# Four-layer graph network, layer 3: a tile's attention logits in one run of four chunks, and another place for ScalarE's second measuring pass

## The chip, the cores and the metric

The kernel runs on one core of a Trainium2 chip, in one launch. The metric is the device time of one execution in microseconds (us), and the profile is that of one execution. The engines are called as in the profile: PE (TensorE's matmuls), PEld (its weight loads), DVE (VectorE), ACT (ScalarE), POOL (GpSimd) and SP (SyncE, which issues most DMAs).

## The reference

`x` is 3327 x 256, `adj` is 3327 x 3327, both float32. Four layers each add `f(relu(layernorm(x)), adj)` to x. Layers 0 to 2 are a plain propagation, a filtered one (tanh, top-k) and a normalised one. The change is in layer 3 alone, which takes two steps of a propagation and of an attention that is cut to the heaviest entries of each row:

```python
def _top_p_attention(X, W1, W2, W3):
    q = X @ W1.T @ W2.T            # 64 wide
    k = X @ W3.T                   # 64 wide
    probs = softmax(q @ k.T)
    # keep, row by row, the largest entries until their sum reaches 0.9
    A = probs * mask
    return A / A.sum(-1)

R = S + I;  R = R / R.sum(-1);  Xf = Xa = X;  Z = 0
for n in range(2):
    A = _top_p_attention(Xa, W1, W2, W3)
    Xf = R @ Xf
    Xa = A @ Xa
    Z = Z + Xf @ U1[n].T + Xa @ U2[n].T
return layernorm(X + Z) * ln_g + ln_b
```

## The kernel before

**Tiles.** The 3327 rows are padded to 3328 = 26 tiles of 128. In each of the two steps a tile passes through four stages.

1. *Logits* (`logits_steps`, L955). The keys lie in two halves of 13 tiles on partitions 0 to 63 and 64 to 127, so a logits matmul has 64-row weights and the two halves are computed by two matmuls side by side. The 13 x 128 = 1664 columns of a half are cut into `CHUNKS` of 512, 512, 512 and 128 (L953). Each chunk has a two-bank buffer of `ps_row` (two such buffers, L80), one bank per half. ScalarE's exp moves it into `e` and gives its sum into a column of `parts` (L983). The steps yield after chunk 1 and after chunk 3, so a tile's logits are two runs on PE.
2. *Search* (`search_steps`, L987). ScalarE sums the parts and works out a first threshold (L1000 to L1005), then measures the row with two passes over 3328 elements: a Relu (L1016) and a Sign (L1021). DVE turns both into a better threshold (L1026 to L1029), measures once more (L1032), collects candidates (L1041 to L1058) and then masks `e` (L1061) and takes the reciprocal `den` (L1065).
3. *Rows times values* (`rows_times_steps`, L177). PE transposes the masked `e` in groups of four blocks (L186) into a buffer of `ps_tr` (two one-bank buffers, L77), ScalarE copies each group to `eT` (L189), and PE multiplies it with the values (L197). `rows.begin` does the first two groups, `rows.finish` the rest.
4. *After the rows.* In step 1 ScalarE scales the result to `xa` (L1223). `turn` transposes it (L146; ScalarE's copy is recorded in `last_copied`), `node` makes the next step's keys and queries from it (L250), and `values` multiplies with U2 (L1236) into a `ps_row` buffer that ScalarE and DVE empty (L1242, `z` L1243). In step 2 ScalarE scales it to `y` (L1308), which POOL adds into z.

**Propagation.** Beside this, PE works off the product of R with the nodes, in phases of 39 or 52 matmuls of 128x128 (L1182; adjacency "slabs" of 832 KB come by DMA, and POOL adds the identity to a diagonal block, L1151). A pair of tiles has two phases.

**What sets the order.** All of this is emitted under `tc.manual_schedule(engines=PE_ALONE)` (L1435): PE's instructions run in the order in which they are emitted, and the Tile scheduler orders the other engines. Emission is steered by plans. A plan is a table from a place to functions; `run(steps, plan)` calls them when the steps have reached that place, and a propagation phase maps the places 0 to 25 onto its 39 or 52 matmuls. The logits of the tile three ahead (`AHEAD`) are hung into such a plan by `spread(steps, first=0, second=10)`, L1492: one run at each of two places. In step 1 most tiles are *interleaved* (a row stage, then a propagation phase; runs at 0 and 12). The tiles in `APART` (3, 7, 11, 15, 19) have no phase of their own, and their plan is that of `rows.finish`, with runs at 4 and 6. The first `EARLY` = 4 phases, and the last ones of step 1 (T - 3, T - 2, T - 1), have places of their own. In step 2 the runs are at 0 and 10 of the phase.

**ScalarE's passes.** `passes_apart` (L1459) puts the first pass (L1016) into `rows.finish` and the second (L1021) into the propagation phase that follows. `tc.issue_after(x)` makes the scheduler put it behind instruction x. The second pass is emitted at place 4 in step 1, behind the last copy of an `xT`, and at place 1 in step 2, behind the last exp issued so far, that is the exp of chunk 1.

Of the kernel before, what the change touches and what calls it, by code (L numbers as in the profile page):

```python
# [11 lines left out]
F32 = mybir.dt.float32  # L12
# [4 lines left out]
AF = mybir.ActivationFunctionType  # L17
# [4 lines left out]
N = 3327  # L22
D = 256
DA = 64
P = 128
T = 26
# [20 lines left out]
def kernel(  # L47
# [22 lines left out]
    nc = tc.nc  # L70
# [6 lines left out]
    ps_tr = ctx.enter_context(tc.tile_pool(name="ps_tr", bufs=2, space=PSUM))  # L77
    ps_acc = ctx.enter_context(tc.tile_pool(name="ps_acc", bufs=2, space=PSUM))

    ps_row = ctx.enter_context(tc.tile_pool(name="ps_row", bufs=2, space=PSUM))  # L80
# [52 lines left out]
    def merged(*plans):  # L133
        out = {}
        for p in plans:
            for k, v in p.items():
                out.setdefault(k, []).extend(v)
        return out

    last_copied, last_turned, last_exp, last_found = [], [], [], []  # L140

    def transposed(src, pool, name):

# [742 lines left out]
    def layer_3_in(tag, big, ep, w3, sm3, h3, kT0, ksum0, left, at_end):  # L886
# [64 lines left out]
            return mean  # L951

        CHUNKS = [(c, min(c + 512, LOW * P)) for c in range(0, LOW * P, 512)]  # L953

        def logits_steps(kT, q, e, name, evict):  # L955


            halves_of_e = e.rearrange("p (h n) -> p h n", h=2)
            for c, (a, b) in enumerate(CHUNKS):
                pl = ps_row.tile([P, 2, 512], F32, tag="row", name=f"pl_{name}_{c}")  # L960
                for h in range(2):
                    nc.tensor.matmul(  # L962
                        pl[:, h, : b - a], q[h * DA : (h + 1) * DA, :], kT[h * DA : (h + 1) * DA, a:b],
                        start=True, stop=True,
                    )
                evict(c, halves_of_e[:, :, a:b], pl[:, :, : b - a])
                if c == len(CHUNKS) - 1:
                    nc.gpsimd.memset(e[:, N:], 0.0)
                if c % 2:
                    yield c  # L970

        def scores(step, m, kT):

            name = f"{tag}{step}_{m}"
            e = ep.tile([P, NP], F32, tag="e", name=f"e_{name}")

            parts = sm3.tile([P, len(CHUNKS) + 1], F32, tag="parts", name=f"parts_{name}")
            nc.gpsimd.memset(parts[:, len(CHUNKS) :], -1.0)
            return e, parts, exp_of_logits(step, m, kT, e, parts)

        def exp_of_logits(step, m, kT, e, parts, name=""):
# [323 lines left out]
        def attention_of_second_step(m, acc, den, name):  # L1305
            y = w3.tile([P, D], F32, tag="xa", name=f"y_{name}")
            with tc.high_priority():
                nc.scalar.activation(y, acc[:, :D], AF.Copy, scale=den)  # L1308
            return y


# [111 lines left out]
        kT1, ksum1 = new_keys(f"1{tag}", big)  # L1423
        AHEAD = 3
# [8 lines left out]
        ORDER = [p + i * H for p in range(H) for i in range(2)]  # L1433

        with tc.manual_schedule(engines=PE_ALONE):  # L1435
# [3 lines left out]
            def prepare(step, m, kT):  # L1439
                made[m] = scores(step, m, kT)  # L1440
                return made[m][2]
# [17 lines left out]
            def passes_apart(step, finder):  # L1459


                if finder is None:
                    return {}, {}

                first = passes(finder)[0]

                def second():
                    with tc.issue_after((last_copied if step == 0 else last_exp)[-1].ins):
                        next(finder, None)
                    next(finder, None)  # L1470

                return {0: first}, {4 if step == 0 else 1: [second]}

            pairs, fs = {}, []

            def propagate_first(n, at):

                p, phase = divmod(n, 2)
                pair = pairs.setdefault(p, PropagatedPair(0, p, h3, ts))
                units = H * len((PHASES if p else FIRST_PHASES)[phase])  # L1480
                run(pair.steps(phase), {k * units // T: v for k, v in at.items()})
                if phase == (p == 0):
                    pair.half()
                if phase and n != T - 3 and n != T - 1:
                    rows_of_first(p)
# [3 lines left out]
                for i in range(2):  # L1489
                    props.append(PropagationOfFirstStep(p + i * H, rows[:, i, :]))  # L1490

            def spread(steps, first=0, second=10):  # L1492

                return {k: [lambda: next(steps, None)] for k in (first, second)}

            class Rows:

# [25 lines left out]
            for i in range(EARLY):  # L1523
                plan = {}
                if props:
                    p = props.pop(0)
                    plan = {6: [lambda: p.scale(last_exp)], 13: [p.turn], 20: [p.sums]}
                if i == 0:
                    left.pool, left.bank = (w3, "eT", 3), one_bank
                    propagate_first(0, dict(zip((20, 25), ([what] for what in left.stages))))  # L1530
                    mean0 = key_sum(kT0, ksum0, "0")
                elif i == 1:
                    steps = prepare(0, 0, kT0)
                    centred = {3: [lambda: centre(kT0, mean0(), "0")]}
                    propagate_first(1, merged(centred, spread(steps, 9, 19), plan))
                    run(find(0, 0, st0))
                else:
                    propagate_first(i, merged(spread(prepare(0, i - 1, kT0)), plan))
                    finder = find(0, i - 1, st0)
                    if i + 1 < EARLY:  # L1540
                        run(finder)
# [3 lines left out]
            propagated = iter(range(EARLY, T - LATE))  # L1545
            for m in range(T):
                interleaved = m + AHEAD < T and m not in APART
                plan, later = passes_apart(0, finder) if interleaved else (passes(finder), {})
                plan = merged(plan, left_over)
                if props:  # L1550
                    p = props.pop(0)
                    plan = merged(plan, {2 if interleaved else 1: [p.scale], 3: [p.turn], 5: [p.sums]})
                steps = iter(())
                if m + AHEAD < T and not interleaved:
                    def begin_logits():
                        nonlocal steps
                        steps = prepare(0, m + AHEAD, kT0)
                        next(steps)

                    plan = merged(plan, {4: [begin_logits], 6: [lambda: next(steps)]})  # L1560
                a = AttentionOfFirstStep(m, rows.finish(m, plan), dens.pop(m), f"{m}")
                if interleaved:
                    left_over = {}
                    steps = prepare(0, m + AHEAD, kT0)
                    after = {3: [a.turn], 9: [a.node], 18: [a.values], 20: [lambda: rows.begin(m + 1)]}
                    propagate_first(next(propagated), merged(spread(steps, 0, 12), after, later))
                elif m == T - 3:
                    left_over = {}
                    after = {1: [a.turn], 4: [a.node], 8: [a.values], 22: [lambda: rows.begin(m + 1)]}
                    propagate_first(T - LATE, after)  # L1570
                elif m + 1 < T:
                    rows.begin(m + 1)
                    a.turn()
                    left_over = {0: [a.node], 2: [a.values]}
                finder = find(0, m + AHEAD, st0) if m + AHEAD < T else None
# [11 lines left out]
            def first_flags():  # L1587
# [4 lines left out]
            steps = prepare(1, 0, kT1)  # L1592
            propagate_first(T - 3, {
                1: [a.turn], 3: [first_flags], 4: [a.node], 8: [a.values, sum_second],
                11: [centre_second], 19: [lambda: next(steps)], 24: [lambda: next(steps)],
            })
            first_e, first_parts = made[0][:2]
            steps_of_second = prepare(1, ORDER[1], kT1)
# [23 lines left out]
        with tc.manual_schedule(engines=PE_ALONE):  # L1622
# [1 line left out]
            run(find(1, 0, st1))  # L1624
            rows_of_first(H - 2)
            p = props.pop(0)
            propagate_first(T - 2, merged(spread(steps_of_second, 0, 6), {3: [lambda: p.scale(last_exp)], 8: [p.turn], 12: [p.sums]}))
            p = props.pop(0)
            second = find(1, ORDER[1], st1)

# [2 lines left out]
                    next(second)  # L1633

            plan = {0: [lambda: p.scale(last_exp)], 3: [p.turn], 8: [p.sums], 15: [lambda: next(second), pass_of_second], 19: [pass_of_second]}
            propagate_first(T - 1, merged(spread(prepare(1, ORDER[2], kT1), 4, 10), plan))
            run(second)
            finder = find(1, ORDER[2], st1)
            fs.append(new_nodes(f"fs{tag}")[:, :, :D])
# [15 lines left out]
            for i, m in enumerate(ORDER):  # L1655
                ahead = ORDER[i + AHEAD] if i + AHEAD < T else None
                plan, later = passes_apart(1, finder) if ahead else (passes(finder), {})
                if i == 0:
                    p, q = props
# [3 lines left out]
                    nc.sync.dma_start(gs, ln_g.partition_broadcast(P))  # L1663
                    nc.sync.dma_start(bs, ln_b.partition_broadcast(P))
                ys[m] = attention_of_second_step(m, acc, dens.pop(m), f"{m}")
                plan = spread(prepare(1, ahead, kT1)) if ahead else {}
                if i + 1 < T:
                    plan = merged(plan, {20: [lambda: rows.begin(ORDER[i + 1])]}, later)
                else:
# [113 lines left out]
```

## Time and profile before

| | |
|---|---|
| median of 3 runs | 2582.86 us (2580.24 to 2583.54) |
| profiled execution | 2582.32 us, of which the span of its instructions is 2580.5 us |
| mean granted PE clock | 0.994 |
| PE, DVE, ACT, POOL busy | 97%, 81%, 42%, 11% of the span |
| logits matmuls in the trace (L962) | 832, from 975.2 to 2482.6 us |
| their two groups' busy time on PE | 88.9 and 87.9 us |
| exps (L983) | 208, 177.8 us on ACT |
| second passes (L1021) | 50, 153.5 us on ACT |

Layers 0 to 2 last until about 960 us of the span. Step 1 of layer 3 follows until about 1850 us, and step 2 to the end.

How to read it: times are counted from the first instruction. A group of instructions is named by line, engine, operation and its operands, "out<-in", with buffer numbers left out. A wait names the instruction that ended it. Successive matmuls overlap in the records, so what a matmul costs PE is read from its start to the next one's start. A float32 matmul appears as two entries of PE.

### The profile page before, as it was taken

The page shows a single profiled execution, that of the slowest core. Times are in us where ns is not written, and L with a number is a line of the kernel's source. Part 1 is how long each engine was busy: PE and PEld are TensorE (multiplying, and loading weights), DVE is VectorE, ACT ScalarE, POOL GpSimd, SP SyncE. Part 2 cuts the span into 40 slices and gives each one's busy share as a digit, 9 for nine tenths or more (in the row PEclk, how much of TensorE's full clock was granted, in tenths as well). Part 3 has the DMA queues.
Part 4 walks back from the last instruction along what each step waited for, and adds up shares of the span by engine and source line. Part 5 has one row for each costly group of instructions (what it writes and reads, how often), then busy time and mean ns, then how long its engine had stood idle before and what let it go on. Part 6 is the DMA issues. An engine that isn't in the chain of part 4 may idle for free. (4 is left out here: it accounts for less than half of the span.)

```text
span 2580.5 us, 47702 instructions
## 1 busy us (share of the span) xinstructions
PE 2514.0 (97%) x17929; PEld 2255.6 (87%) x17929; DVE 2082.3 (81%) x5538; ACT 1083.7 (42%) x2055; POOL 293.1 (11%) x485
## 2 busy tenths in 40 slices
PE   7999999999999999999999999998999999999997
PEld 7999999999999998878787878787888888888886
DVE  6667788888878778787778787784899899899994
ACT  3110123343111115555656566653555555555551
POOL 2000010000000001000000000000021122212132
PEclk9999999999999999999999999999999999999999
DMA  6677765555788865323232323232433343344342
GB/s 222 191 227 249 220 197 182 166 173 171 250 294 269 280 208 186 107 65 107 69 103 92 107 67 102 61 113 97 159 119 106 112 135 111 112 141 130 106 135 84
DMA packets 181794, 388.47 MB, mean 151 GB/s; under 512 B 19742, under 2 KB 78747, under 8 KB 181531
## 3 DMA queue, kind: packets, MB, share of 16 engines
q1 hardware_dynamic: 153210, 364.31, 43.7%
q10 hardware_dynamic: 28320, 20.80, 2.5%
q8 instruction: 147, 2.41, 0.4%
q14 instruction: 117, 0.95, 0.1%
HBM read 315.44 MB, written 67.89 MB: 149 GB/s over the span
## 5 line engine op out<-in xcount | busy, mean ns | idle before, releaser
L189 ACT COPY eT_a<-pt_a 128x512 f32<-128x512 f32 (+1 forms) x364 | 195.8, 554 | 361.2 <-PE pt_a L186 361.0
L197 PE MATMUL a<-h3a,eT_a 128*128 128x256 f32 x1352 | 325.7, 383 | 0.2 <-ACT eT_a L189 0.2
L197 PE MATMUL a<-vs,eT_a 128*128 128x256 f32 x1352 | 320.3, 381 | 0.2 <-ACT eT_a L189 0.2
L1045 DVE MAX8 cand_a<-w 128x8 f32<-128x128 f32 x1352 | 290.0, 279 | 4.5
L197 PEld LDWEIGHTS a<-h3a,eT_a 128*128 128x128 f32 x1352 | 245.7, 191 | 37.5 <-issue 5.7
L197 PEld LDWEIGHTS a<-vs,eT_a 128*128 128x128 f32 x1352 | 244.7, 190 | 30.2 <-ACT eT_a L189 0.7
L557 PE MATMUL acc_a<-tsa,s_a 128*128 128x128 f32 (+1 forms) x2028 | 269.1, 275 | 0.0
L557 PE MATMUL acc_a<-rhs,a_a 128*128 128x128 f32 (+1 forms) x2028 | 251.4, 277 | 0.1
L557 PE MATMUL acc_a<-tsa,a_a 128*128 128x128 f32 x2028 | 250.3, 275 | 0.9 <-DVE tsa L351 0.9
L557 PEld LDWEIGHTS acc_a<-tsa,s_a 128*128 128x128 f32 x2028 | 248.2, 192 | 0.3
L557 PEld LDWEIGHTS acc_a<-rhs,a_a 128*128 128x128 f32 x2028 | 239.3, 192 | 2.2 <-ACT rhs L436 0.4
L557 PEld LDWEIGHTS acc_a<-tsa,a_a 128*128 128x128 f32 x2028 | 239.1, 192 | 2.1 <-DVE tsa L351 1.3
L1041 DVE SCALAR_TENSOR_TENSOR w<-e_a,t_a 128x896 f32<-128x896 f32 x208 | 225.0, 1082 | 4.4
L983 ACT ACTIVATE e_a<-pl_a 128x1024 f32<-128x1024 f32 x208 | 177.8, 860 | 108.6 <-PE pl_a L962 108.6
L186 PE MATMUL pt_a<-ident,e_a 128*128 128x128 f32 x1352 | 199.9, 274 | 6.9 <-DVE e_a L1061 6.6
L186 PEld LDWEIGHTS pt_a<-ident,e_a 128*128 128x128 f32 x1352 | 165.9, 141 | 36.5 <-DVE e_a L1061 7.2
L1151 POOL TENSOR_TENSOR slab3a<-slab3a,ident 128x128 f32<-128x128 f32 x100 | 104.2, 1043 | 814.5 <-DMA slab3a<-in_adj_t_dram 379.1
L1061 DVE SCALAR_TENSOR_TENSOR e_a<-e_a,all_least 128x3328 f32<-128x3328 f32 x52 | 194.4, 3739 | 1.8
L1032 DVE SCALAR_TENSOR_TENSOR w<-e_a,t_a 128x3328 uint8<-128x3328 f32 x52 | 191.7, 3686 | 4.0
L395 ACT ACTIVATE xT_a<-pt_a 128x512 f32<-128x512 f32 x52 | 30.8, 593 | 356.6 <-PE pt_a L391 300.5
L1182 PEld LDWEIGHTS f0a<-tsa,slab3a 128*128 128x128 f32 x1352 | 160.2, 192 | 16.9 <-issue 13.9
L688 ACT ACTIVATE a_a<-a_a 128x640 f32<-128x640 f32 (+1 forms) x156 | 101.4, 665 | 174.2 <-DVE a_a L687 152.9
(246 smaller groups left out, 4224.2 us busy)
## 6 DMA issues: line engine op xcount, KB each, us to landing
slab3a<-s_dram SPq DMA_DIRECT2D x100, 832.0 KB, 4.6
a_a<-in_adj_t_dram SPq DMA_DIRECT2D x312, 256.0 KB, 4.1
slab3a<-in_adj_t_dram SPq DMA_DIRECT2D x79, 832.0 KB, 4.6
a_a<-in_adj_t_dram SPq DMA_DIRECT2D x156, 320.0 KB, 3.8
s_dram<-s_a SPq DMA_DIRECT2D x78, 256.0 KB, 4.9
s_dram<-s_a SPq DMA_DIRECT2D x39, 320.0 KB, 5.2
x_dram<-x_a ACTq DMA_DIRECT2D x39, 256.0 KB, 3.5
s_dram<-a_a SPq DMA_DIRECT2D x26, 256.0 KB, 5.2
```

The lines of the kernel that those rows point to most:

```text
L186: nc.tensor.transpose(pt[:, j, :], e[:, k * P : (k + 1) * P], ident)
L189: last_turned.append(nc.scalar.copy(eT[:, : len(blocks), :], pt[:, : len(blocks), :]))
L197: nc.tensor.matmul(acc[:, :width], ready[g][:, j, :], rhs[:, k, :], start=(k == 0), stop=(k == T - 1))
L557: nc.tensor.matmul(self.acc[:, g, at : at + wide], quads[n][:, k - CUTS[c][0], :], t, start=(k == 0 and n in (1, 4)), stop=(k == H - 1 and ...
L688: nc.scalar.activation(a, a, AF.Tanh)
L983: last_exp.append(nc.scalar.activation(dst, src, AF.Exp, accum_out=parts[:, c : c + 1]))
L1032: nc.vector.scalar_tensor_tensor(junk, e, t, e, ALU.is_lt, ALU.mult, accum_out=got)
L1041: nc.vector.scalar_tensor_tensor(w[:, : (b - a) * P], eg, t, eg, ALU.is_lt, ALU.mult, accum_out=below[:, g : g + 1])
L1045: nc.vector.max(cand[:, 8 * k : 8 * k + 8], w[:, (k - a) * P : (k - a + 1) * P])
L1061: nc.vector.scalar_tensor_tensor(e, e, least, e, ALU.is_ge, ALU.mult, accum_out=st["kept"][:, m : m + 1])
L1151: nc.gpsimd.tensor_tensor(x[:, p, :], x[:, p, :], ident, ALU.add)
L1182: nc.tensor.matmul(self.accs[bank][:, c * P : (c + 1) * P], a, self.right(n, k), start=start, stop=last.get(bank) == (n, k), skip_group_ch ...
```

## The change

`logits_steps` now issues all four chunks in one run and yields once at its end. Chunk 2 goes into two buffers of `ps_tr`, one bank per half, and is emptied by two exps of 512 columns; the other chunks still use `ps_row`, one exp each. `parts` has one column more. The memset of the last column of `e` follows the run.

`spread` gives way to `whole_run(steps, at)`, which puts the run at one place: 9 and then 3 in the early phases (9 and 19, then 0 and 10, before), 10 in the interleaved phases of step 1 (0 and 12), 4 in the rows of the APART tiles (4 and 6), 20, 0 and 4 in the last three phases of step 1 (19 and 24, 0 and 6, 4 and 10), and 7 in step 2 (0 and 10).

In step 2 the second pass is emitted at place 0 instead of 1, behind the last `y` (recorded in `last_scaled`) instead of the last exp.

```diff
         CHUNKS = [(c, min(c + 512, LOW * P)) for c in range(0, LOW * P, 512)]
+        IN_TURNED = 2
+        PIECES = len(CHUNKS) + 1
...
             halves_of_e = e.rearrange("p (h n) -> p h n", h=2)
+            n = 0
             for c, (a, b) in enumerate(CHUNKS):
-                pl = ps_row.tile([P, 2, 512], F32, tag="row", name=f"pl_{name}_{c}")
+                if c == IN_TURNED:
+                    pls = [ps_tr.tile([P, 4, P], F32, tag="tr", name=f"pl_{name}_{c}_{h}") for h in range(2)]
+                    parts = [pl.rearrange("p j n -> p (j n)")[:, : b - a] for pl in pls]
+                else:
+                    pl = ps_row.tile([P, 2, 512], F32, tag="row", name=f"pl_{name}_{c}")
+                    parts = [pl[:, h, : b - a] for h in range(2)]
                 for h in range(2):
                     nc.tensor.matmul(
-                        pl[:, h, : b - a], q[h * DA : (h + 1) * DA, :], kT[h * DA : (h + 1) * DA, a:b],
+                        parts[h], q[h * DA : (h + 1) * DA, :], kT[h * DA : (h + 1) * DA, a:b],
                         start=True, stop=True,
                     )
-                evict(c, halves_of_e[:, :, a:b], pl[:, :, : b - a])
-                if c == len(CHUNKS) - 1:
-                    nc.gpsimd.memset(e[:, N:], 0.0)
-                if c % 2:
-                    yield c
+                if c == IN_TURNED:
+                    for h in range(2):
+                        evict(n, halves_of_e[:, h, a:b], parts[h])
+                        n += 1
+                else:
+                    evict(n, halves_of_e[:, :, a:b], pl[:, :, : b - a])
+                    n += 1
+            nc.gpsimd.memset(e[:, N:], 0.0)
+            yield 0
...
-                nc.scalar.activation(y, acc[:, :D], AF.Copy, scale=den)
+                last_scaled.append(nc.scalar.activation(y, acc[:, :D], AF.Copy, scale=den))
...
-                    with tc.issue_after((last_copied if step == 0 else last_exp)[-1].ins):
+                    with tc.issue_after((last_copied if step == 0 else last_scaled)[-1].ins):
                         next(finder, None)
                     next(finder, None)
 
-                return {0: first}, {4 if step == 0 else 1: [second]}
+                return {0: first}, {4 if step == 0 else 0: [second]}
...
-            def spread(steps, first=0, second=10):
-
-                return {k: [lambda: next(steps, None)] for k in (first, second)}
+            def whole_run(steps, at):
+
+                return {at: [lambda: next(steps)]}
...
-                    propagate_first(1, merged(centred, spread(steps, 9, 19), plan))
+                    propagate_first(1, merged(centred, whole_run(steps, 9), plan))
...
-                    propagate_first(i, merged(spread(prepare(0, i - 1, kT0)), plan))
+                    propagate_first(i, merged(whole_run(prepare(0, i - 1, kT0), 3), plan))
...
-                    plan = merged(plan, {4: [begin_logits], 6: [lambda: next(steps)]})
+                    plan = merged(plan, {4: [lambda: next(prepare(0, m + AHEAD, kT0))]})
...
-                    propagate_first(next(propagated), merged(spread(steps, 0, 12), after, later))
+                    propagate_first(next(propagated), merged(whole_run(steps, 10), after, later))
...
-                11: [centre_second], 19: [lambda: next(steps)], 24: [lambda: next(steps)],
+                11: [centre_second], 20: [lambda: next(steps)],
...
-            propagate_first(T - 2, merged(spread(steps_of_second, 0, 6), {3: [lambda: p.scale(last_exp)], 8: [p.turn], 12: [p.sums]}))
+            propagate_first(T - 2, merged(whole_run(steps_of_second, 0), {3: [lambda: p.scale(last_exp)], 8: [p.turn], 12: [p.sums]}))
...
-            propagate_first(T - 1, merged(spread(prepare(1, ORDER[2], kT1), 4, 10), plan))
+            propagate_first(T - 1, merged(whole_run(prepare(1, ORDER[2], kT1), 4), plan))
...
-                plan = spread(prepare(1, ahead, kT1)) if ahead else {}
+                plan = whole_run(prepare(1, ahead, kT1), 7) if ahead else {}
```

More of the change, by code (lines that the diff above doesn't have):

```diff
@@ L138, in merged @@
         return out
-    last_copied, last_turned, last_exp, last_found = [], [], [], []
+    last_copied, last_turned, last_exp, last_found, last_scaled = [], [], [], [], []
     def transposed(src, pool, name):
@@ L975, in scores @@
             e = ep.tile([P, NP], F32, tag="e", name=f"e_{name}")
-            parts = sm3.tile([P, len(CHUNKS) + 1], F32, tag="parts", name=f"parts_{name}")
-            nc.gpsimd.memset(parts[:, len(CHUNKS) :], -1.0)
+            parts = sm3.tile([P, PIECES + 1], F32, tag="parts", name=f"parts_{name}")
+            nc.gpsimd.memset(parts[:, PIECES:], -1.0)
             return e, parts, exp_of_logits(step, m, kT, e, parts)
@@ L1552, in layer_3_in @@
                     plan = merged(plan, {2 if interleaved else 1: [p.scale], 3: [p.turn], 5: [p.sums]})
-                steps = iter(())
                 if m + AHEAD < T and not interleaved:
[L1555 to L1558, printed above, removed]
-                    plan = merged(plan, {4: [begin_logits], 6: [lambda: next(steps)]})
+                    plan = merged(plan, {4: [lambda: next(prepare(0, m + AHEAD, kT0))]})
                 a = AttentionOfFirstStep(m, rows.finish(m, plan), dens.pop(m), f"{m}")
```

## The prediction, as it went on record

> **What bounds the kernel now.** I began with the page's busy times, since they say which engine the time must come from.
>
> ```profile
> PE 2514.0 (97%) x17929; PEld 2255.6 (87%) x17929; DVE 2082.3 (81%) x5538; ACT 1083.7 (42%) x2055; POOL 293.1 (11%) x485
> ```
>
> PE is busy for 97% of the span. In layer 3 it stands still for hardly anything: the windows of step 2 (1870 to 2480 us) show 609.9 of 610 us busy. So the kernel can shorten in two ways only: PE's own stream gets cheaper, or one of its few stalls goes. The timeline of PE shows what a tile's logits cost in that stream (start, length, with runs of like matmuls put together).
>
> ```profile
> 2083.11 0.38 PE L1182 MATMUL f1a<-fsa,slab3a 128*128 128x128 f32 x2
> 2083.43 1.99 PE L962 MATMUL pl_a<-kT_1a,qT 64*128 64x512 f32 x8
> 2085.34 4.73 PE L1182 MATMUL f1a<-fsa,slab3a 128*128 128x128 f32 x40
> ...
> 2090.00 1.35 PE L962 MATMUL pl_a<-kT_1a,qT 64*128 64x512 f32 x8
> 2091.28 1.38 PE L1182 MATMUL f1a<-fsa,slab3a 128*128 128x128 f32 x10
> ```
>
> From start to next start, chunks 0 and 1 hold PE 1.915 us, chunks 2 and 3 hold it 1.28 us. The starts of the single matmuls say what of this is columns. Inside a run a pair of half-matmuls follows the last after 0.429 us (512 columns) or 0.109 us (128). But the first pair takes 0.533, the last one 0.095 to 0.10 more than its pitch, and the steps from the 128x128 stream into the run and out of it take 0.205 and 0.213 us where that stream's pitch is 0.112. Each run thus pays 0.10 + 0.10 + 0.09 + 0.10 = 0.39 us that no column explains.
>
> The waits come next, first PE's, then DVE's and the weight loads' (waiter <- releaser: us, times, longest).
>
> ```profile
> PE pt_a L186 <- DVE e_a L1061: 6.6, 3, 2.4
> PE pl_a L962 <- DVE z L1243: 2.8, 3, 0.9
> PE f1a L1182 <- DMA slab3a<-in_adj_t_dram: 2.5, 1, 2.5
> ...
> DVE u_a L1026 <- ACT junk_a L1021: 132.1, 28, 8.3
> ...
> PEld pl_a L962 <- issue: 45.1, 180, 3.3
> ```
>
> The first three are nearly all of PE's stalls in this layer. The fourth says that DVE, 81% busy in all, loses 132 us waiting for ScalarE's second measuring pass; it matters because DVE's mask (L1061) releases the first. The last is the weight load's side of the toll on logits runs: it waits for nothing that the profile names. A window row (PE, PEld, DVE, ACT, POOL busy, clock) adds what a stall costs beyond itself:
>
> ```profile
> 1018.00:1020.40 2.40, 0.02 (x1) 0.03 (x1) 2.40 (x3) 0.00 (x0) 0.00 (x0) 1.00 0.60 128
> 1022.00:1025.50 3.50, 3.50 (x11) 2.74 (x11) 3.50 (x17) 0.14 (x1) 1.38 (x1) 0.51 0.06 22
> ```
>
> After 2.4 us without matmuls the granted clock was 0.51 for 3.5 us: eight matmuls of L197 took 3.44 us there, 1.73 to 1.9 elsewhere.
>
> [...] The logits use 64-row weights, all around them 128-row ones; [...] with 0.09 to 0.10 us more on either side of a run. [...] 1.02 us for 1024 elements, 0.38 for 256, hence 0.833 ns each and 0.17 fixed.
>
> **The change, part by part.**
>
> *One run instead of two.* Merged, the run takes 0.533 + 5 x 0.429 + 0.109 + 0.208 = 2.995 us instead of 1.915 + 1.28 = 3.195, and one pair of entry and exit goes: 0.19. That is 0.39 us a tile, on PE's path; 26 tiles x 2 steps = 52: **-20.3 us**. The built order has 52 runs of four chunks where there were 104.
>
> *What ScalarE pays, and chunk 3's buffer.* Chunk 3 reuses the row buffer of chunk 0, and is due 0.53 + 5 x 0.43 = 2.68 us after the run starts. The exp of chunk 0 starts 1.17 us after it (2083.43 to 2084.60) and takes 1.02, so the buffer is free at about 2.2. The margin is 0.4 us. I cost this at nothing in step 2; what hides it is that ScalarE is free at that point. The critical case is the new second pass. It now stands right behind y (L1308):
>
> ```profile
> 2083.31 0.47 ACT L1308 ACTIVATE y<-a,den_a 128x256 f32<-128x256 f32 x1 [2.17 <-PE a L197]
> 2084.60 1.02 ACT L983 ACTIVATE e_a<-pl_a 128x1024 f32<-128x1024 f32 x1 [0.82 <-PE pl_a L962]
> ...
> 2086.61 3.07 ACT L1021 ACTIVATE junk_a<-e_a,t_a 128x3328 uint8<-128x3328 f32 x1
> ```
>
> y ends 0.67 us after PE has begun the phase, so the pass occupies 0.67 to 3.73. At place 7 of a 39-matmul phase the run begins after 11 matmuls, 2.55 us in. Exp 0 could start at 3.73, and does at about 3.75; it ends at 4.78, chunk 3 is due at 5.23. In the 52-matmul phase the run begins at 3.45, later still. If this cover were gone, each us of lateness beyond 0.4 costs PE one us per tile. In step 1 the pass stands behind the copy of xT as before, with kT, qT, a DMA issue (0.47 us) and then the exps; I allow **+0.7** for small stalls there. Chunk 2 now costs two exps of 512: I take 0.60 each from the fit above, between 0.51 (half of 1024) and 0.7. That is 0.17 us more per tile, on an engine at 42%: nothing. The transposes that next want those banks come over 4 us after the run in every place I followed in the order; so nothing. A memset (POOL) and a sixth column of parts weigh nothing on PE.
>
> *Step 1's other places.* In the three tiles after an APART tile chunk 1 waits for z (L1243) to leave its row buffer: such a run holds PE 3.11 us instead of 1.92. At place 10 of the interleaved phase that z is long done: 3 x 1.19 = **-3.6**.
>
> *The mask waits (L186 <- L1061).* (1) At 1018, 2.57 us and then half the clock for 3.4 us, about 1.4 lost. Tile 0's chunks 2 and 3 now come 4 to 5 us earlier in the phase, and its search with them. All of it would be 4.0; bounds 0 and 4.0, taken **-3.0**. (2) At 1258 and 1498, tiles 7 and 15, 2.3 and 2.1 us and one half-clock spell of some 1.8. DVE's timeline shows why the mask is late:
>
> ```profile
> 1253.37 3.68 DVE L1032 SCALAR_TENSOR_TENSOR w<-e_a,t_a 128x3328 uint8<-128x3328 f32 x1
> ...
> 1256.98 3.68 DVE L1061 SCALAR_TENSOR_TENSOR e_a<-e_a,all_least 128x3328 f32<-128x3328 f32 x1
> ```
>
> A later tile's measuring sum (L1032) goes ahead of the mask that PE needs. In the built order of the change these masks come first, 3.7 us earlier than now against a wait of 2.3. In all 6.2; bounds 0 and 6.5, taken **-5.2**. Two APART tiles also wait 0.6 and 0.5 us at L146, behind exps that are now earlier: **-0.3**.
>
> *Step 2 and the tail.* A pair of phases is 55.94 us of PE now and 55.16 after. DVE needs about 54.4 of it by its timeline, of which 1.5 are the wait for the pass (it ends 2119.07 now; at phase start + 3.73, near 2116.4, after: before DVE asks for it at 2117.7). So this wait goes, DVE keeps over 2 us a pair, and it is not late at the end. The last slab's DMA is issued at 2533.28, behind SP's waits for z, which comes late out of DVE and POOL; PE stands 2.6 us for it. DVE ahead by some 2.8 us issues it earlier: bounds 0 and 2.6, **-2.0**. SP's load of one slab moves behind one z load, with some 13 us in hand, and POOL's diagonal add for tile 13 behind three z operations, some 1 us in hand: nothing. If they were late, 1 us each, once.
>
> *New loss.* At 1848, the change of steps, PE waits 1.27 us for ScalarE's scales, and a short pass now goes ahead of two copies: **+0.8**.
>
> The sum: -20.3 - 3.6 - 3.0 - 5.2 - 0.3 - 2.0 + 0.7 + 0.8 = -32.9. The profiled execution took 2582.32 (span 2580.5 and 1.8 around it), so 2549.4; the median shown is 0.5 above it: **2550**.
>
> **The rivals.**
>
> *Only the toll goes.* The stalls are each set by a chain of several engines; another link may be just as late. Then -20.3 - 3.6 + 1.5: **2560**. For it: three of my terms are waits of one or two occurrences, read from an order and not from a run. Against it: every link I traced moves the same way.
>
> *ScalarE takes the saving (slower).* The new second pass, 3.07 us, stands ahead of exp 0, and the margin in the 39-matmul phase is 0.4 us. If exp 0 starts s us later than I place it, PE stalls s - 0.4 at chunk 3 in each tile. From s = 1.05 (0.65 x 52 = 33 us) nothing is left, from 1.15 it is slower by the 5 us that can be told. With s = 1.4: 2550 + 52 = **2602**. For it: ScalarE works in order, and step 1 puts several copies there as well. Against it: the pass needs only numbers that ScalarE itself made long before, and y follows PE's own end in the timeline (no wait but PE's), so nothing seems able to push it. Small s, in some tiles, is likelier: 2555 to 2577.
>
> *DVE becomes the bound of step 2.* If the pass doesn't take away its wait, DVE needs 54.4 of 55.16, and one more us a pair gives 0.3 x 12.5 = 4 us back, with the tail's 2: **2556**.
>
> *The order isn't what the diff says.* The built order excludes that: one run per tile, and the pass behind y.
>
> **How the numbers follow.** Forecast (2546 to 2554): 0.68. Only the toll (2557 to 2563): 0.17. DVE bound: 0.05. ScalarE takes part: 0.05, of which half ends at the level of before. ScalarE takes all and more: 0.05. A measurement of this kernel can tell about 0.2%, 5 us, from no change: faster 0.92, same 0.03, slower 0.05. The range goes from 2543 (every wait at its best bound and no new loss: -39) to 2566 (only the toll, and some lateness of exp 0).
>
> **What would show it.** Right: 52 runs of L962's successor, each 3.0 us from start to next start; the weight loads' issue wait about halved from 45 us; no PE wait on L1243; DVE's wait for the second pass in step 2 near zero; the slab of the tail issued before PE asks. Wrong: PE waits at chunk 2 or 3 for ScalarE's exp, masks still late at the APART tiles, or a run longer than 3.2 us, where the toll would have been something that merging doesn't save.

## The result, and the profile after

The changed kernel takes 2552.71 us (median of 4 runs, 2549.34 to 2553.21) against 2581.82 us for the kernel before on the same chip (four runs of it now, three in the table above). The ratio is 0.9888, 95% interval 0.9873 to 0.9902: 29 us less, 25 to 33 by the interval. The forecast was 2550. The profiled execution took 2549.34 us, span 2547.5 us. The changed kernel's exp is L995, its logits matmuls L970; other lines of layer 3 are 12 higher than before.

Not all of the 33 us between the two spans is the change. Layer 3's first propagation matmul starts at 956.0 us in the profile before and at 950.4 in the one after, and the layers ahead of it are untouched. In all ten profiles of this study it starts somewhere between 949.7 and 956.0. So I compare layer 3 alone, from that matmul on, by the starts of PE's matmuls (us):

| stretch of layer 3 | before | after | difference |
|---|---|---|---|
| to the first product of row tile 0 (L197) | 65.7 | 62.1 | -3.6 |
| the rows of step 1, to row tile 0 of step 2 | 816.1 | 799.6 | -16.5 |
| first two row tiles of step 2 | 63.8 | 62.9 | -0.9 |
| next 22 row tiles of step 2 | 612.3 | 605.2 | -7.1 |
| last two, to PE's last matmul | 50.4 | 52.6 | +2.2 |
| from there to the end | 16.1 | 14.6 | -1.5 |
| sum | 1624.4 | 1597.0 | -27.4 |

The page after, to set beside the line of before:

```profile
PE 2491.6 (98%) x17929; PEld 2255.1 (89%) x17929; DVE 2091.2 (82%) x5538; ACT 1086.9 (43%) x2159; POOL 309.2 (12%) x485
```

PE executes as many matmuls and is busy 22 us less. Its timeline in step 2 shows the run that replaces the two of before (start, length, engine, line):

```profile
2113.26 0.72 PE L1194 MATMUL f1a<-fsa,slab3a 128*128 128x128 f32 x5
2113.91 3.07 PE L970 MATMUL pl_a<-kT_1a,qT 64*128 64x512 f32 x16
2116.91 1.27 PE L1194 MATMUL f1a<-fsa,slab3a 128*128 128x128 f32 x9
```

From start to next start it is 3.00 us, as worked out. From the list of PE's waits after (us in total, times, longest):

```profile
PE f1a L1194 <- DMA slab3a<-in_adj_t_dram: 3.0, 1, 3.0
PE pl_a L970 <- DVEq L1419: 2.5, 1, 2.5
...
PE f1a L1194 <- POOL parts_a L990: 1.3, 1, 1.3
```

The waits for masks (6.6 us before) and for z (2.8) are gone. The one for the tail's slab is still there, and one for POOL is new. From the waits of the other engines:

```profile
DVE u_a L1038 <- ACT junk_a L1033: 100.9, 21, 7.7
...
PEld pl_a L970 <- issue: 39.6, 160, 2.8
...
PEld pl_a L970 <- ACT e_a L995: 20.5, 52, 0.6
...
PEld pl_a L970 <- ACT qT L262: 12.4, 18, 1.2
```

DVE waits 31 us less for the second pass. Chunk 2's exps of 512 elements take 0.60 us each (mean of 104), as the prediction estimated from ScalarE's exps of 1024 and 256 elements before (1.02 and 0.38 us). The third line is chunk 3's weight load waiting for chunk 0's exp, 0.4 us in each of the 52 tiles. PE itself doesn't stand for it. In step 2 chunk 3 starts 0.48 us after that exp's end, and where it does stall (place 4 below) 0.14 us after it, so 0.34 us are left of the margin that the prediction put at 0.4. The last line belongs to a loss that I had put too low (below).

### The profile page after: what moved, and what is told of

It is laid out like the page before. It is cut to its first block, busy times and chain, and to the rows that moved or that the text cites. A ratio compares the mean times of both kernels' runs of the same rounds, so it can differ in the third digit from the quotient of the medians.

```text
span 2547.5 us, 47851 instructions
## 1 busy us (share of the span) xinstructions
PE 2491.6 (98%) x17929; PEld 2255.1 (89%) x17929; DVE 2091.2 (82%) x5538; ACT 1086.9 (43%) x2159; POOL 309.2 (12%) x485
## 5 line engine op out<-in xcount | busy, mean ns | idle before, releaser
L197 PE MATMUL a<-h3a,eT_a 128*128 128x256 f32 x1352 | 323.5, 381 | 0.2 <-ACT eT_a L189 0.2
L197 PE MATMUL a<-vs,eT_a 128*128 128x256 f32 x1352 | 320.4, 381 | 0.2 <-ACT eT_a L189 0.2
L197 PEld LDWEIGHTS a<-h3a,eT_a 128*128 128x128 f32 x1352 | 244.2, 189 | 33.8 <-issue 2.6
L197 PEld LDWEIGHTS a<-vs,eT_a 128*128 128x128 f32 x1352 | 244.7, 190 | 30.3 <-ACT eT_a L189 0.7
L995 ACT ACTIVATE e_a<-pl_a 128x1024 f32<-128x1024 f32 x260 | 184.7, 728 | 43.3 <-PE pl_a L970 37.1
L186 PE MATMUL pt_a<-ident,e_a 128*128 128x128 f32 x1352 | 199.5, 273 | 0.2
L1163 POOL TENSOR_TENSOR slab3a<-slab3a,ident 128x128 f32<-128x128 f32 x100 | 92.0, 921 | 861.9 <-DMA slab3a<-in_adj_t_dram 336.1
L1044 DVE SCALAR_TENSOR_TENSOR w<-e_a,t_a 128x3328 uint8<-128x3328 f32 x52 | 192.1, 3695 | 4.3
L1073 DVE SCALAR_TENSOR_TENSOR e_a<-e_a,all_least 128x3328 f32<-128x3328 f32 x52 | 191.9, 3691 | 1.9
L186 PEld LDWEIGHTS pt_a<-ident,e_a 128*128 128x128 f32 x1352 | 166.3, 141 | 29.3 <-ACT eT_a L189 2.6
L1194 PE MATMUL f0a<-tsa,slab3a 128*128 128x128 f32 x1352 | 166.5, 277 | 0.0
```

The lines of the kernel that those rows point to most:

```text
L186: nc.tensor.transpose(pt[:, j, :], e[:, k * P : (k + 1) * P], ident)
L197: nc.tensor.matmul(acc[:, :width], ready[g][:, j, :], rhs[:, k, :], start=(k == 0), stop=(k == T - 1))
L995: last_exp.append(nc.scalar.activation(dst, src, AF.Exp, accum_out=parts[:, c : c + 1]))
L1044: nc.vector.scalar_tensor_tensor(junk, e, t, e, ALU.is_lt, ALU.mult, accum_out=got)
L1073: nc.vector.scalar_tensor_tensor(e, e, least, e, ALU.is_ge, ALU.mult, accum_out=st["kept"][:, m : m + 1])
L1163: nc.gpsimd.tensor_tensor(x[:, p, :], x[:, p, :], ident, ALU.add)
```

## The experiments

Eight kernels. The first four ran on one chip (before: 2580.74 us), the other four on another (2581.34). Where two are a few us apart, I read the stretch of the trace that the edit touches, since the first 950 us alone vary by 6.

**Two runs again, in step 2 only.** After chunk 1 the steps yield, and two propagation matmuls later chunks 2 and 3 follow. All buffers and exps are those of the changed kernel.

```diff
+                if split and c == 1:
+                    yield c
...
-                plan = whole_run(prepare(1, ahead, kT1), 7) if ahead else {}
+                plan = two_runs(prepare(1, ahead, kT1, True), 7, 8) if ahead else {}
```

> The changed kernel, but in step 2's main loop (23 tiles) the logits stop after chunk 1 and go on after two or three propagation matmuls (places 7 and 8). Nothing else moves. If the gain in step 2 is the toll of a run (0.39 us each), 23 x 0.39 = 9.0 us come back: 2552.7 + 9.0 = 2561.7, and PE's 28-us stretch from tile to tile is 0.39 us longer with no new wait. If the gain came from waits that the new places took away, nothing comes back: 2552.7, since the places stay.

Measured: 2556.39 us, ratio 0.9908 (0.9891 to 0.9925). PE's timeline of it:

```profile
2119.95 1.99 PE L970 MATMUL pl_a<-kT_1a,qT 64*128 64x512 f32 x8
2121.87 0.71 PE L1196 MATMUL f1a<-fsa,slab3a 128*128 128x128 f32 x4
2122.51 1.35 PE L970 MATMUL pl_a<-kT_1a,qT 64*128 64x512 f32 x8
2123.79 2.27 PE L1196 MATMUL f1a<-fsa,slab3a 128*128 128x128 f32 x18
```

A pair of tiles takes 55.935 us here, 55.933 in the kernel before and 55.145 in the changed one (mean of 8 pairs). So 0.79 us a pair, 0.39 a tile, is the toll of the second run and nothing else. The time rose by less than 9 us because two waits shrank: the last stretch is 3.2 us shorter, with a wait for the slab of 1.4 us instead of 3.0 and no half clock after it, and the wait of 1.3 us for POOL is gone. The rival (no toll) falls.

The toll doesn't come from changing between any two groups of matmuls either. In step 2 of the kernel before, a step from the propagation (L1182) to the transposes (L186) or to the products (L197) takes 0.112 us, the propagation's own pitch, and the step from a transpose back takes 0.109, the transposes' own. These all have 128-row weights. Only the step to the 64-row logits takes 0.205.

**The second pass behind the run.** In step 2 the pass is emitted at place 8, behind the run's last exp.

```diff
-                    with tc.issue_after((last_copied if step == 0 else last_scaled)[-1].ins):
+                    with tc.issue_after((last_copied if step == 0 else last_exp)[-1].ins):
...
-                return {0: first}, {4 if step == 0 else 0: [second]}
+                return {0: first}, {4 if step == 0 else 8: [second]}
```

> The changed kernel, but in step 2 the second pass is emitted at place 8, behind the last exp of the run, as before the change it stood behind the last exp issued so far. The pass then ends about 10 to 11 us after the phase starts instead of 3.7. If DVE is close to the bound there, it waits 4 to 5 us for the pass in one phase of a pair and 1 to 2 in the other, needs 58 to 60 us a pair against PE's 55.2, and PE waits for masks: 3 to 4 us x 11.5 pairs = 35 to 45 us, 2588 to 2598. If the pass's place is of no weight (DVE has slack enough): 2553, within 3 us.

Measured: 2563.50 us, ratio 0.9936 (0.992 to 0.9953). PE's waits from 1850 to 2480 us:

```profile
PE pt_a L186 <- DVE e_a L1073: 3.5, 5, 1.9
PE pt_a L186 <- ACT t_a L1017: 2.8, 6, 0.5
```

PE waits at the transposes in each pair, and 5.8 us before the last but one row tile. The second line names ACT, but the mask came last there too: at one such wait it ended at 2131.72, and the transposes began at 2131.87. In every pair the masks of one tile end 0.15 us before its transposes. So the direction is right: with this place DVE is the bound, at about 55.76 us a pair. The size was wrong by a factor of three or more. DVE's wait for the pass, in ten pairs (1880 to 2440 us):

```profile
DVE u_a L1038 <- ACT junk_a L1033: 21.0, 10, 2.5
```

That is 2.1 a pair and not 6, so I estimate that it needs 55.76 - 2.1 = 53.7 us without this wait. The pass behind y instead of behind the run is worth about 11 us, but only once the runs are merged (see the pass alone).

**Chunk 2 in a row buffer.** All four chunks share the two `ps_row` buffers, and chunk 2 has one exp.

```diff
-        IN_TURNED = 2
-        PIECES = len(CHUNKS) + 1
+        IN_TURNED = None
+        PIECES = len(CHUNKS)
```

> The changed kernel, but chunk 2 uses a two-bank row buffer like the others, with one exp of 1024 elements, so all four chunks share two buffers. If the buffer decides, chunk 2 is due 1.83 us after the run's start and chunk 0's exp has ended only at about 2.2 to 2.3: it stalls 0.4 to 0.5 us, and chunk 3 then waits a little for chunk 1's exp; with what the restart of the stream costs 0.5 to 0.8 us a tile, x 52 = 26 to 42 us: 2579 to 2595, the whole gain or more. If the transposes' banks are not needed: 2553 or less.

Measured: 2586.72 us, ratio 1.0028 (1.0016 to 1.0039): the gain is gone. PE's timeline shows the run broken in the middle:

```profile
2145.16 1.99 PE L970 MATMUL pl_a<-kT_1a,qT 64*128 64x512 f32 x8
2147.50 1.50 PE L970 MATMUL pl_a<-kT_1a,qT 64*128 64x512 f32 x8 [0.36 <-ACT e_a L995]
```

34 of the 52 runs take 3.77 us instead of 3.00, the others more, 44 us in all over the changed kernel's runs. Layer 3 as a whole is only 34.6 us longer, because other places are shorter, the last stretch by 3.6. The transposes' banks are what lets the run go through without a stall.

**Step 1's run two places later.**

```diff
-                    propagate_first(next(propagated), merged(whole_run(steps, 10), after, later))
+                    propagate_first(next(propagated), merged(whole_run(steps, 12), after, later))
```

> The changed kernel with the interleaved tiles' run at place 12 of their phase instead of 10. In the changed kernel nine of these runs take 3.35 or 3.67 us instead of 3.00, chunk 1 waiting for the row buffer from which ScalarE still copies the keys and queries behind its second pass. If that is the cause, all runs take 3.00 and 4.4 us go: 2548.3. The masks for the tiles after an APART tile have 3.7 us in hand and come about 0.7 us later: no loss. If the wait is for ScalarE in general (its exps), the nine stay long: 2552.7.

Measured: 2547.21 us, ratio 0.9876 (0.9859 to 0.9893). The times alone don't tell it from the changed kernel. The runs do: 50 of 52 take 3.00 us, where in the changed kernel nine took 3.35 or 3.67, and the rows of step 1 are 4.1 us shorter. The same stretch of PE in it:

```profile
1446.28 0.61 PE L250 MATMUL pkq<-xT_a,kq 128*128 128x128 f32 x4
1446.73 1.28 PE L1194 MATMUL f0a<-tsa,slab3a 128*128 128x128 f32 x10
1447.94 3.07 PE L970 MATMUL pl_a<-kT_0a,qT 64*128 64x512 f32 x16
```

**The pass alone.** The kernel before with the second pass at place 0 behind y, and nothing else.

```diff
-                    with tc.issue_after((last_copied if step == 0 else last_exp)[-1].ins):
+                    with tc.issue_after((last_copied if step == 0 else last_scaled)[-1].ins):
...
-                return {0: first}, {4 if step == 0 else 1: [second]}
+                return {0: first}, {4 if step == 0 else 0: [second]}
```

> The kernel before, with one part of the change alone: step 2's second pass at place 0, behind y. DVE's wait for it (1.5 us a pair) should go. PE sets the pace there and waited for no mask in step 2, so nothing follows: 2581, within 3 us (the tail's slab may come up to 2.6 us sooner). If DVE were the bound of step 2, 1.5 x 11.5 pairs = 17 us would go: 2564.

Measured: 2579.43 us, ratio 0.9994 (0.9985 to 1.0003). A pair takes 55.934 us as before: DVE was not the bound of step 2. Its wait for the pass didn't go, though: 9.9 us between 1880 and 2440 us, against 12.1. In the tiles where it waits, DVE now asks for the pass 2.3 to 2.8 us after y starts instead of 5.0: it seems to have run ahead as far as the pass allowed. With both changes the wait is 1.2.

**Step 2's run at place 4.**

```diff
-                plan = whole_run(prepare(1, ahead, kT1), 7) if ahead else {}
+                plan = whole_run(prepare(1, ahead, kT1), 4) if ahead else {}
```

> The changed kernel with step 2's run at place 4 instead of 7, so that the run begins before the second pass is over. If chunk 3 hangs on chunk 0's exp and that on the pass, exp 0 starts 3.75 us into the phase whatever the place, and ends at 4.78; chunk 3 is due at 1.43 + 2.68 = 4.11 in the 39-matmul phase and at 4.56 in the 52-matmul one: stalls of 0.67 and 0.22, each with 0.1 for the restart, 1.1 us a pair, 12 us in all: 2564. If the margin is larger than worked out: 2553. The steps 1 of both are alike.

Measured: 2555.14 us, ratio 0.9893 (0.9876 to 0.9909). A pair takes 55.80 us, 0.66 more. Of its two runs one takes 3.10 us and the other 3.55. PE's wait in the longer ones:

```profile
PE pl_a L970 <- ACT e_a L995: 2.8, 10, 0.3
```

That is the expected stall in the expected phases, smaller by 0.2 us each, and my counting is to blame: place 4 lets 7 and 9 matmuls go ahead of the run, not 6 and 8, which is 0.22 us. Put right, the expectation is a stall of 0.44 and none, with 0.1 for the restart 0.54 and 0.1; measured are 0.55 and 0.10. So the slower rival's mechanism is real, and place 7 lies just clear of it.

**A third buffer for x3.** The tag is shared with step 1's hT, so both have three.

```diff
-            x3 = w3.tile([P, NC, P], F32, tag="hT", name=f"x3_{name}").rearrange("p c n -> p (c n)")
+            x3 = w3.tile([P, NC, P], F32, tag="hT", name=f"x3_{name}", bufs=3).rearrange("p c n -> p (c n)")
```

> The changed kernel with three buffers instead of two for the x3 loads of the output (and what shares their tag). In the changed kernel PE waits 3.1 us in the last phase for a slab whose load SP holds behind an x3 load, that waits for the z of the last but one tile; half-clock matmuls after it cost 1.6 more. If that chain is the cause, the slab is issued 3.4 us sooner, and both go: 4.7 us, 2548.0. If the slab itself is late (its buffer, or the DMA queue), nothing goes: 2552.7.

Measured: 2548.47 us, ratio 0.9877 (0.986 to 0.9893). The time is near what was expected, but the trace doesn't bear the reason out:

```profile
2498.40 3.51 PE L1194 MATMUL f1a<-tsa,slab3a 128*128 128x128 f32 x30
2504.50 1.55 PE L186 MATMUL pt_a<-ident,e_a 128*128 128x128 f32 x8 [2.59 <-DVE e_a L1073]
```

The slab now comes in time. PE stands as long at nearly the same point, for the last mask. The last stretch is 0.5 us shorter and not 4.7. What else differs lies within what varies from profile to profile, so I count no gain.

**Both.** Place 12 and three x3 buffers.

> The changed kernel with both: step 1's run at place 12 and three x3 buffers. The two are in different stages, so they add: 2552.7 - 4.6 - 4.7 = 2543.4. If they don't, it is the tail that fails, and the time is that of place 12 alone, 2547.

Measured: 2543.62 us, ratio 0.9858 (0.9841 to 0.9874), the best of the study. It is 38 us below before and some 8 below the changed kernel; the intervals of these two just touch. Layer 3 is 7.2 us shorter than in the changed kernel: 3.0 in the rows of step 1, 2.7 in the last stretch, 1.4 elsewhere. So the expected sum was met, but not by its terms (4.6 and 4.7). The last stretch still has a wait for the mask, of 2.1 us instead of 3.1 for the slab. That is 1.0 of the 2.7. The other 1.7 is a half clock that did not come: from 2500.2 to 2503.0 the granted clock was 1.00 here, and 0.59 after the stall in the changed kernel and in the one with the third buffer alone. I can't say that it stays away in every execution.

## Why the prediction was right, and where it wasn't

**Right: the toll.** -20.3 us was taken for 52 x 0.39. In step 2 the pair periods give 0.394 a tile, and the two-run kernel gives it back exactly. In step 1 it wasn't tried apart, but the undisturbed runs have the same lengths there: 1.92 and 1.28 us before, 3.00 after. It is three quarters of layer 3's 27 us. That it goes with the change between 128-row and 64-row weights fits the steps shown above (0.205 us into the 64-row logits, 0.112 and 0.109 between 128-row groups); no run has logits with 128-row weights. One sign was read wrongly: I expected the weight loads' issue wait to halve from 45 us, and it is 39.6. Most of that wait stands inside runs and isn't what merging saves.

**Right: the masks.** -3.0 and -5.2 were taken, bounded by 4.0 and 6.2; the waits at the first row tile and at tiles 8 and 16, with their half-clock matmuls, are all gone. (The prediction lists the last two under tiles 7 and 15, whose stage they stand in; the masks are those of 8 and 16.) DVE's timeline shows the mask ahead of the measuring sum, as the order had it:

```profile
1237.91 3.69 DVE L1073 SCALAR_TENSOR_TENSOR e_a<-e_a,all_least 128x3328 f32<-128x3328 f32 x1
...
1242.59 3.69 DVE L1044 SCALAR_TENSOR_TENSOR w<-e_a,t_a 128x3328 uint8<-128x3328 f32 x1
```

The mask ends at 1241.6, 3.7 us before PE's transposes at 1245.30. No run here separates the merging of the runs from their new places. Against the first row tile's share stands a new wait of 0.9 us at 1022.5 for ScalarE's xf (L1268), which I had not seen.

**Wrong in size: step 1's chunk 1.** The step "I allow +0.7 for small stalls there" was 4.4. The three waits for z (-3.6) did go, but nine others came: five runs of 3.35 and four of 3.67 us. PE's and ScalarE's timelines of the changed kernel at one of them:

```profile
1447.59 0.61 PE L250 MATMUL pkq<-xT_a,kq 128*128 128x128 f32 x4
...
1448.58 1.13 PE L970 MATMUL pl_a<-kT_0a,qT 64*128 64x512 f32 x4
1450.04 2.28 PE L970 MATMUL pl_a<-kT_0a,qT 64*128 64x512 f32 x12 [0.34 <-ACT qT L262]
```

```profile
1446.05 3.07 ACT L1033 ACTIVATE junk_a<-e_a,t_a 128x3328 uint8<-128x3328 f32 x1
...
1449.23 0.27 ACT L258 ACTIVATE kT_1a<-pkq 64x128 f32<-64x128 f32 x1
...
1449.73 0.26 ACT L262 COPY qT<-pkq 64x128 f32<-64x128 f32 x1
```

PE computes the keys at 1447.6 into a row buffer. ScalarE empties it only after its 3.07 us pass, at 1450.0, and chunk 1, one place behind the keys, needs that very buffer. In the runs of 3.35 us the same copy ends less late (1067.86 for a run that began at 1066.70). Two places more cure it, which place 12 shows. I had treated ScalarE's queue as a question of when exps start, not of who holds the second row buffer.

**Wrong: "SP's load ... and POOL's diagonal add ...: nothing. If they were late, 1 us each, once."** The load was in time. The add was late, and cost 1.2 us more than at the same place before. POOL's timeline:

```profile
1898.15 3.71 POOL L1163 TENSOR_TENSOR slab3a<-slab3a,ident 128x128 f32<-128x128 f32 x1 [0.91 <-DMA slab3a<-in_adj_t_dram]
```

The step was right about the place and the size, but "nothing" was wrong, and the reason, DVE (last section), was not in it. The pass alone brought it too: 1.5 us at 1922.6 in that kernel.

**Wrong: the tail, -2.0.** "DVE ahead by some 2.8 us issues it earlier" failed. In the built order DVE's additions of the last pair (L1214) stand one group of candidates later: 14.4 us after the mask ahead of them, where it had been 12.1. That costs more than DVE had won. Counted from the moment at which PE starts its last matmul before the slab, that mask ends 0.5 us sooner than in the kernel before, and the slab is issued 0.9 us later. The chain that ended last, in the changed kernel:

```profile
2499.34 0.74 POOL z L1310
2500.10 0.32 SPq L1292
2500.51 4.71 DMA slab3a<-in_adj_t_dram
2505.26 0.84 PE f1a L1194 x4
```

PE stood 3.1 us instead of 2.6, and this time the granted clock fell after it, as the window rows of the changed kernel show in the column behind POOL's:

```profile
2502.30:2505.20 2.90, 0.00 (x0) 0.00 (x0) 2.87 (x4) 0.00 (x0) 2.89 (x1) 1.00 0.87 311
2505.20:2508.00 2.80, 2.74 (x14) 2.74 (x15) 1.43 (x7) 0.69 (x2) 0.90 (x2) 0.59 1.06 435
```

In the kernel before it had stayed at 1.00:

```profile
2538.40:2541.00 2.60, 2.54 (x23) 2.55 (x24) 1.33 (x6) 1.07 (x2) 0.80 (x2) 1.00 1.00 409
```

The stretch became 2.2 us longer, 0.5 by the stall and 1.7 by the clock. And the wait has two chains behind it. In the changed kernel the last mask ended at 2505.06 and the slab landed at 2505.22, while PE needs the mask only four matmul entries after the slab. So an earlier slab could bring PE's transposes from 2505.89 to 2505.06 and no further, and the third x3 buffer shows just that. It was so before as well: mask at 2538.15, slab at 2538.41, transposes at 2539.00. Of the 2.6 us at most 0.85 could have gone by the slab alone, and reading the mask's end would have told. How much goes when both are early wasn't tried.

**The rest.** The last 1.5 us, after PE's last matmul, are gone in the changed kernel and in every one made from it (14.0 to 14.6 us against 16.1 and 16.3). They lie behind the kernel's own work: the last output lands at 2572.2 us before and at 2540.9 after, and from there to the end of the span it is 8.2 and 6.5 us. I can't say what that stretch consists of. The rival "only the toll goes" (2560) fell on the masks but was right about the tail. DVE as the bound of step 2 appears where the pass is late. ScalarE's rival appears at place 4.

Added up: -20.3 - 3.6 + 4.4 - 4.0 + 0.9 - 6.2 - 0.5 (L146) + 1.2 + 2.2 - 1.5 + 0.4 (the change of steps) = -27.0, against -27.4 in the table. The forecast had -32.9. So that 2550 came within 3 us of the median is in part luck: the terms that came out worse than forecast (small stalls, the tail, POOL, xf) add up to 10.0 us, those that came out better (masks, change of steps, L146, the unexplained end) to 4.1, and the layers ahead, which are as they were, differ by up to 6 us from profile to profile.

## What to carry to other kernels

Here each run of 64-row matmuls amid 128-row ones cost 0.39 us beyond its columns, for the longer run and the shorter one alike. In such a stream count the runs, not only the columns, and look for a bank elsewhere that lets two runs become one. Before a wait is counted as gain, read the time at which every other input of the waiting instruction is ready; two chains that end within 0.3 us of each other are one wait with two causes. When an instruction stands behind a long pass on its engine, ask which buffer it holds, and who needs that next.

## What the hardware showed that I had not expected

POOL's identity add of 128x128 takes 0.46 us, but 3.71 at 1898, while DVE ran its measuring sum (L1044) from 1897.86 to 1901.54. In the changed kernel's layer 3, 23 of the 31 adds that took over 0.8 us overlap a DVE pass over 3328 elements (22 times L1044, once L1073), and each of these ends 0.3 us after it. Both lines read `e` as both of their tensor operands. An add at 979.73, inside a DVE pass over the same 3328 elements that reads `e` once (L1031), took 0.46 us. That is one add, so whether the second operand makes the difference was not shown.

The half clock didn't follow from a stall's length alone: it came after 2.4 us (at 1018 before), 2.3 (at 1258 before: granted clock 0.50 from 1261.0 to 1264.4) and 3.0 us (at 2502 after), and stayed away after 2.0 us (at 1498 before: 1.00 from 1500.7 to 1506.0) and 2.5 (at 2536 before). What else decides it, no run here shows.
